# Layer 0 of a convolution-attention kernel: the matrix of scores times ones, by VectorE or by one-column products on TensorE

## The chip, the cores and the metric

One core of one Trainium2 chip. The metric is the device time of one execution in microseconds (us); lower is better. The kernel before takes 2922.1 us, the median of 3 runs (2920.12 to 2923.42).

## The reference, cut to what matters

The model has two layers. Layer 0 is a spectral convolution with attention between the 32 channels ("times") of each of 4 batches; layer 1 is additive attention over tokens and a small mixture of experts. Only a corner of layer 0 is touched:

```
p_attn = jax.nn.softmax(scores, axis=-1)              # (b, head n, t, s)
av = jnp.einsum('bnts,bnsk->bntk', p_attn, vf)        # vf: spectral part + skip part of the values
p = _fno_layer(av, Pcw, Psw, H, W)                    # mixes the 32 heads again
```

Values and the output projection each have a spectral part and a "skip" part, a plain scale per head (`Vsw[n]`, `Psw[n]`). The skip of the skip needs no spectrum: with the per-head product `pv[n] = Vsw[n] * Psw[n]`, image t receives from image s the factor sum over n of `pv[n] * p_attn[n, t, s]`, times the normalization scale of image s. This 32 x 32 matrix of the scores, summed over heads, plus a unit diagonal (the residual `p + xa`), is what the changed function makes. It is applied to the pixels of image s as a product.

## The kernel before, in words

**The stages of layer 0.** The kernel runs layer 0 for 4 batches b (each 32 images of 128 x 128), then layer 1. For each b the order is: the convolution loop (line 963 on), the transform back, statistics, two spectral layers with a GELU, and, still within b, the attention weights of batch b+1 and the last additions of b.

**The convolution loop.** Five blocks of up to 13 rows of modes (`x0`), each with four groups of source images (`i`), so 20 steps per b. Each step loads `xb` by DMA from SyncE's queue (SP) into a ring of four buffers, copies it to PSUM as `xw` on ScalarE (L980), makes four products `u`: one or two on GpSimd (L989, SBUF with SBUF), the rest on VectorE (L993, PSUM with SBUF), in a ring of six buffers (tag `pr`), and TensorE sums them with the scores `pr` into `po` (L926), in the order in which they were made. Between the steps TensorE turns pixels (`pxt`), ScalarE normalizes them (`xq`), and `skip` multiplies them by `bd` (`sk`, L926 too): the first use of `bd`, some 10 us after the loop begins.

**The end of a batch.** `attention_weights(b + 1, ...)` ends in the softmax and the normalized scores `ph` (L755 on GpSimd, 64 partitions: 32 heads for each half of the times). They go to DRAM and back as `pr`. Meanwhile the last additions of batch b run: for each half `a` of the images, `row_products` makes `y` on TensorE (L342), ScalarE copies it as `v` (L356), TensorE makes `four` (L358, two PSUM buffers, tag `b`) and VectorE adds it to the images `x` (L1399). Then x1, the output of the layer, is stored (L1422), and the loop of b+1 begins.

**The function that is changed**, `skip_matrix` (L780), makes `bd` from `ph`. It is called once before the loop over b (for batch 0) and after the first half (`a == 0`) of the last additions for b = 0, 1 and 2. It does this:
- `sel` (L238): a 0/1 matrix `same` that picks partition p's own image, times the normalization scale.
- `cm` (L787): for each half of the times, one product of 32 rows by 512 columns with `pv` broadcast as the weights, so that all 128 partitions get sum over heads of `pv * ph` for every pair (s, t).
- `cd` (L791) and `cp` (L792): VectorE multiplies the 512 columns by `sel` and sums over s, which leaves each partition the row of its own s.
- `cp` (L795): plus `same`. `bd` (L797): spread over four blocks by a mask.

**What sets the order.** A scheduler places the instructions on each engine by its own estimates; `behind(later, earlier)` pins one instruction after another on the same engine. `cm` is pinned behind `inverted`, the last product of the first half. [...]Rings (tags `a`, `b`, `v`, `wide`, `pr`) say which buffers are shared: `cm` is in PSUM tag `a` (two buffers), as are the `po` of the loop; `cd` shares tag `v` (three buffers) with the copies `v`.

Of the kernel before, what the change touches and what calls it, by code (L numbers as in the profile page):

```python
# [7 lines left out]
F32 = mybir.dt.float32  # L8
AF = mybir.ActivationFunctionType
ALU = mybir.AluOpType  # L10
AX = mybir.AxisListType
PSUM = bass.MemoryType.PSUM

P = 128
B, T, H, C = 4, 32, 128, 128
NH = 32
# [20 lines left out]
def _constants():  # L37

    w = np.arange(P)
    kx = np.concatenate([np.arange(32), np.arange(-32, 0)])  # L40
    ky = np.arange(KY)
    th = 2 * np.pi / P
    c, s = np.cos(th * np.outer(w, kx)), np.sin(th * np.outer(w, kx))
    rows = np.concatenate([c, -s], 1)
    inv_rows = np.concatenate([c.T, -s.T], 0)
    angle = th * np.outer(w, ky)
    cc, cs = np.cos(angle), np.sin(angle)

    cols = np.concatenate([cs, 0 * cc[:, :1], cc, cc[:, 32:33], -cs], 1) / NPIX
    along_c = np.concatenate([cc[:, 1:], cs[:, 1:], -cs[:, 1:]], 1) / NPIX  # L50
    twice = np.where(ky == 0, 1.0, 2.0)[:, None]
    re, im = twice * cc.T, -twice * cs.T
    inv_cols = np.concatenate([re, im], 0)
    back = np.tile(2 * np.concatenate([cc.T[1:], cs.T[1:]], 1), (4, 1))
    p = np.arange(P)
    same = (p[:, None] % 32 == np.arange(32)[None, :]).astype(np.float64)
    block = (p[:, None] // 32 == np.arange(4)[None, :]).astype(np.float64)

    eye = np.eye(32)
    comb = np.zeros((4, 32, 3, 32))  # L60
    comb[0, :, 0], comb[3, :, 0] = eye, -eye
    comb[1, :, 1], comb[2, :, 1] = eye, eye
    comb[:, :, 2] = -comb[:, :, 0]
    pairs = np.concatenate([np.tile(eye, (4, 1)), np.concatenate([eye, eye, -eye, -eye])], 1)

    of_cos, of_sin = np.zeros((2, 2, 32, 2, KX))
    k = np.arange(1, 32)
    of_cos[0, 0, 0, 0] = 1
    of_sin[0, 0, 1, 0] = -1
    for m, sign in ((k, 1), (KX - k, -1)):  # L70
        of_cos[0, k, 0, m], of_cos[1, k, 1, m] = 1, sign
        of_sin[1, k, 0, m], of_sin[0, k, 1, m] = sign, -1
    low = np.r_[0:16, 48:64]
    unfold = [
        np.concatenate([-t[:, 1, low], t[:, 0, low], t[:, 1, low], t[:, 0], t[:, 1]], 1)
        for t in (of_cos.reshape(KX, 2, KX), of_sin.reshape(KX, 2, KX))
    ]
    unfold = np.tile(np.concatenate(unfold, 1), (2, 1))
    high = ((p % KX >= 16) & (p % KX < 48)).astype(np.float64)
    edge = np.zeros(P)  # L80
    edge[:KY] = edge[KY + 2 : 2 * KY] = 1
    edge[0] = edge[KY - 1] = 0.5
    no_column = np.where(p % KX == 16, 0, high / 2)
    of_low = np.where(p >= KX, 1, np.where(p % 32 == 16, 1, 0.5))
    halves = np.stack([high, no_column, edge, of_low], 1)

    group = (p[:, None] // 4 == p[None, :] // 4) / (4.0 * NPIX / C * T)
    of_group = p[:, None] // 4 == np.arange(32)[None, :]
    by_p = np.concatenate(
        [rows, inv_rows, cols, unfold, halves, same, block, comb.reshape(P, 96), pairs, group, of_group / 4]  # L90
        + [along_c, back],
        1,
    )
    return by_p.astype(np.float32), inv_cols.astype(np.float32)


NX = 2 + 3 * KY
NU = 3 * 32 + 2 * KX
NY = KY - 1
NCONST = 128 + 128 + NX + 2 * NU + 4 + 32 + 4 + 96 + 64 + P + 32 + 3 * NY + 2 * P  # L100
NM = KX * KY
NK = 13

# [27 lines left out]
def layer0(  # L131
# [12 lines left out]
    def behind(later, earlier):  # L144

        tc.add_manual_dep(
            later.ins,
            earlier.ins.name,
            mybir.DependencyInfo(mybir.DependencyClass.NoSync, mybir.DependencyReason.DATA),
            reason="order",  # L150
        )
# [25 lines left out]
    def columns(n):  # L177
        at[0] += n
        return cst[:, at[0] - n : at[0]]
# [8 lines left out]
    group, of_group = columns(P), columns(32)  # L188
    cos_c, sin_c, minus_sin_c = columns(NY), columns(NY), columns(NY)
    cos_back, sin_back = columns(P), columns(P)  # L190
    par = const.tile([P, NSMALL], F32, name="par")
    nc.sync.dma_start(out=par, in_=small_row.partition_broadcast(P))
    ident = const.tile([P, P], F32, name="ident")
# [35 lines left out]
    def per_image(name):  # L229
        return small.tile([P, T], F32, name=name, tag=name)  # L230

    def scalars(op, name, a, b):

        out = per_image(name)
        if isinstance(b, float) or b.shape[1] == 1:
            nc.vector.tensor_scalar(out, a, b, None, op)
        else:
            nc.vector.tensor_tensor(out, a, b, op)  # L238
        return out
# [94 lines left out]
    def row_products(spec, a, ahead=(), slots=range(4), wide=None):  # L334

        wide = wide or [ps.tile([P, 2, 512], F32, name="y1", tag="wide") for _ in range(2)]
        for slot in slots:
            c = slice(slot * P, slot * P + P)
            for k, trig in enumerate((cos_back, sin_back)):
                for g in range(4):  # L340
                    r = slice(32 * g, 32 * g + 32)
                    mm = nc.tensor.matmul(  # L342
                        wide[g // 2][:, g % 2, c],
                        spec[r, 4 * a + slot, 64 - 64 * k : 192 - 64 * k],
                        trig[r],
                        start=k == 0,
                        stop=k == 1,
                    )
                    for earlier in ahead:
                        behind(mm, earlier)  # L350
        return wide

    def four_images(wide, g, copy, v_ring=dict(tag="v", bufs=3), tag="b"):
# [32 lines left out]
    def one(name, n=1):  # L386
        return small.tile([P, n], F32, name=name, tag=name)
# [391 lines left out]

    def skip_matrix(ph, ysc, earlier=None):  # L780

        cp = per_image("cp")
        sel = scalars(ALU.mult, "sel", same, ysc)
        for h in range(2):
            r = slice(32 * h, 32 * h + 32)
            cm = ps.tile([P, T, 16], F32, name="cm", tag="a")
            mm = nc.tensor.matmul(cm, pv[r].to_broadcast([NH, P]), ph[r], start=True, stop=True)  # L787
            if earlier is not None:
                behind(mm, earlier)
            cd = grp.tile([P, T, 16], F32, name="cd", tag="v", bufs=3)  # L790
            nc.vector.tensor_tensor(cd, cm, sel.unsqueeze(2).to_broadcast([P, T, 16]), ALU.mult)  # L791
            nc.vector.tensor_reduce(  # L792
                cp[:, 16 * h : 16 * h + 16], cd.rearrange("p s t -> p t s"), AX.X, ALU.add
            )
        nc.vector.tensor_add(cp, cp, same)  # L795
        bd = small.tile([P, 4, T], F32, name="bd", tag="bd")
        nc.vector.tensor_tensor(  # L797
            bd,
            block.unsqueeze(2).to_broadcast([P, 4, T]),
            cp.unsqueeze(1).to_broadcast([P, 4, T]),  # L800
            ALU.mult,
        )
        return bd
# [108 lines left out]
    for b in range(B):  # L912
# [480 lines left out]
        for a in HALVES:  # L1393
            groups = [slice(16 * a + g, 16 * a + g + GI) for g in (0, GI)]

            def last(images, four):
                g = images[0] - 16 * a
                to = xr[:, 16 * a : 16 * a + 16].rearrange("p (k t) c -> p k t c", k=2)[:, :, g : g + 2]
                added = nc.vector.tensor_tensor(to, to, four.rearrange("p (k t) c -> p k t c", k=2), ALU.add)  # L1399
                if a == 0:  # L1400
                    behind(added, weights[7])

            def last_scaled(images, four):
                for j, t in enumerate(images):
                    nc.scalar.activation(
                        gl[:, t],
                        four[:, j],
                        AF.Identity,
                        bias=cq[:, t : t + 1],
                        scale=c3[:, t : t + 1],  # L1410
                    )
                for t in (images[0], images[2]):
                    nc.vector.tensor_tensor(xr[:, t : t + 2], xr[:, t : t + 2], gl[:, t : t + 2], ALU.add)

            if b + 1 < B:
                inverted = back(spec, a, last, begun if a == 0 else (), nc.scalar.copy)
            else:
                back(spec, a, last_scaled, apart=True)
            if a == 0 and b + 1 < B:
                bd = skip_matrix(weights[2], front[4], inverted)  # L1420
            for i in groups:
                stored = nc.sync.dma_start(out=x1[b, i].rearrange("t w c -> w t c"), in_=xr[:, i])  # L1422
                if b + 1 < B:
                    behind(stored, weights[3])
# [639 lines left out]
```

## Time and profile before

| | us |
|---|---|
| median of 3 runs | 2922.1 |
| profiled execution, device time | 2926.9 |
| its span in the trace | 2925.1 |
| loop of the first batch, first to last `u` of VectorE | 70.52 to 130.36 |
| loop of the second batch | 267.58 to 323.03 |
| loop of the third batch, start | 458.87 |
| loop of the fourth batch, start | 650.37 |
| `cm` products | 16 records, median 0.640 |
| `cd` | 8, median 0.687 |
| `cp` sums | 8, median 1.022 |
| `cp` plus `same` | 4, 0.179 to 2.067 |
| `bd` | 4, 0.279 to 1.978 |

Everything in layer 0 lies before about 836 us; layer 1 takes the rest. Times in the trace are from the start of the span. One float32 product of the program shows as two records (the 8 `cm` products are 16 records). A row of the timeline gives start, length, engine, line, operation, output and inputs, count, and in brackets how long the engine had been idle and what ended that.

### The profile page before, as it was taken

What the parts mean: (1) busy time and instruction counts of PE and PEld (TensorE: products, weight loads), DVE (VectorE), ACT (ScalarE), POOL (GpSimd) and SP (SyncE); (2) the same over time, 40 slices, a digit from 0 to 9 for tenths busy, and PEclk for the clock granted to TensorE, in tenths of its full rate; (3) what the DMA queues carried; (4) which work ended last, traced back from release to release, by engine and by line L of the source; (5) the groups of instructions that cost most, each with busy time, mean ns of one, the idle gap of its engine ahead of it and who ended that gap; (6) DMA issues with size and microseconds to landing.
All of it is one profiled execution on the core that took longest, in us unless ns stands there. A gap on an engine that the chain in (4) does not pass through costs nothing.

```text
span 2925.1 us, 52645 instructions
## 1 busy us (share of the span) xinstructions
PE 2735.4 (94%) x19506; PEld 1352.7 (46%) x19506; DVE 2189.4 (75%) x4860; ACT 2322.9 (79%) x3243; POOL 2034.0 (70%) x1804
## 2 busy tenths in 40 slices
PE   8898998988878999999899999989999999999997
PEld 5565664655544444334444443434444343444443
DVE  4888788778756777666587787657778776878877
ACT  3556466455469999899899999989999998999991
POOL 1706418146139887878988887898787889798773
PEclk9999999999979999999999999999999999999998
DMA  3304205033020101011000100210000011000000
GB/s 101 123 1 112 78 15 163 13 75 101 19 77 9 25 8 33 8 33 41 19 8 17 24 15 17 49 27 14 24 17 15 19 48 26 15 19 15 15 15 15
DMA packets 151152, 107.71 MB, mean 37 GB/s; under 512 B 36302, under 2 KB 140017, under 8 KB 150897
## 3 DMA queue, kind: packets, MB, share of 16 engines
q1 hardware_dynamic: 147633, 102.26, 13.1%
q8 instruction: 154, 2.52, 0.4%
q10 hardware_dynamic: 3264, 2.10, 0.3%
q14 instruction: 101, 0.83, 0.1%
HBM read 63.86 MB, written 19.50 MB: 28 GB/s over the span
## 4 chain that ended last, share of the span: by engine, by line
PE 47%; POOL 11%; ACT 9%; issue 5%; DVE 5%; DMA 0%; POOLq 0%; SPq 0%; DVEq 0%; ACTq 0%
PE d L1854 20%; PE po L1873 12%; PE px L1760 6%; ACT r L1904 5%; PE n L1854 4%; POOL e L1913 3%; POOL e L1912 3%; ACT e L1920 2%; POOL kx L1519 1%; DVE r L1909 1%; DVE xc L1764 1%; POOL x L1519 1%; PE pl L1738 1%; POOL u L989 1%; ACT r L1916 1%
## 5 line engine op out<-in xcount | busy, mean ns | idle before, releaser
L1909 DVE TENSOR_TENSOR r<-n,r 128x1024 f32<-128x1024 f32 (+1 forms) x1056 | 962.0, 953 | 481.5 <-PE n L1854 397.9
L1912 POOL TENSOR_TENSOR e<-r 128x512 f32<-128x512 f32 x528 | 673.2, 1275 | 273.3 <-DVE r L1909 272.8
L1904 ACT ACTIVATE r<-d 128x1024 f32<-128x1024 f32 (+1 forms) x1056 | 792.9, 802 | 67.4 <-PE n L1854 59.3
L1916 ACT ACTIVATE r<-r 128x1536 f32<-128x1536 f32 x528 | 783.6, 1484 | 16.8
L1913 POOL TENSOR_TENSOR e<-e,r 128x512 f32<-128x512 f32 x528 | 671.3, 1271 | 41.4
L1854 PE MATMUL d<-qe,ke 32*128 32x512 f32 (+3 forms) x2304 | 607.5, 603 | 39.9 <-ACT r L1904 35.8
L1873 PE MATMUL po<-e,kx 128*128 128x512 f32 (+3 forms) x1152 | 594.3, 605 | 17.2 <-POOL e L1925 17.2
L1854 PE MATMUL n<-qe,ke 32*128 32x512 f32 (+3 forms) x2304 | 607.0, 602 | 0.0
L1854 PE MATMUL n<-qf,kf 32*128 32x512 f32 (+3 forms) x2304 | 553.5, 555 | 0.0
L1854 PE MATMUL d<-qf,kf 32*128 32x512 f32 (+3 forms) x2304 | 551.9, 555 | 0.0
L1764 DVE SCALAR_TENSOR_TENSOR xc<-px,wgt,xc 128x128 f32<-128x128 f32 x1024 | 358.4, 351 | 41.4 <-PE px L1760 10.6
L1920 ACT ACTIVATE e<-e 128x512 f32<-128x512 f32 x528 | 325.8, 617 | 66.0 <-POOL e L1913 65.1
L1873 PEld LDWEIGHTS po<-e,kx 128*128 128x128 f32 x1152 | 175.4, 188 | 394.6 <-issue 308.6
L1854 PEld LDWEIGHTS d<-qe,ke 32*128 32x128 f32 x2304 | 177.0, 184 | 360.2 <-ACT r L1904 340.2
L1854 PEld LDWEIGHTS d<-qf,kf 32*128 32x128 f32 x2304 | 220.7, 186 | 177.2 <-issue 164.5
L1760 PE MATMUL px<-we,x2t 128*128 128x512 f32 x512 | 265.9, 605 | 6.8 <-DVE xc L1764 5.5
L989 POOL TENSOR_TENSOR u<-xb,gb 128x858 f32<-128x858 f32 (+1 forms) x112 | 220.5, 2008 | 42.6 <-PE po L926 38.8
L1854 PEld LDWEIGHTS n<-qf,kf 32*128 32x128 f32 x2304 | 228.4, 185 | 18.9 <-issue 11.2
L1140 POOL TENSOR_TENSOR spec<-part,part 128x512 f32<-128x512 f32 x16 | 25.8, 1610 | 286.5 <-DVE gn_r_t L253 93.1
L993 DVE TENSOR_TENSOR u<-xw,gb 128x858 f32<-128x858 f32 (+1 forms) x208 | 215.4, 1100 | 6.8 <-ACT xw L980 3.2
L1854 PEld LDWEIGHTS n<-qe,ke 32*128 32x128 f32 x2304 | 177.9, 183 | 9.4 <-DVE r L1909 0.9
L926 PE MATMUL po<-u,pr 128*32 128x429 f32 (+1 forms) x1280 | 151.2, 532 | 24.9 <-POOL u L989 18.5
(425 smaller groups left out, 3378.4 us busy)
## 6 DMA issues: line engine op xcount, KB each, us to landing
xb<-xd SPq DMA_DIRECT2D x128, 214.5 KB
xc<-x SPq DMA_DIRECT2D x29, 512.0 KB
x<-x SPq DMA_DIRECT2D x16, 512.0 KB
qf<-qe SPq DMA_DIRECT2D x64, 128.0 KB
out<-xc SPq DMA_DIRECT2D x15, 512.0 KB
x<-in_x SPq DMA_DIRECT2D x14, 512.0 KB
xb<-xd SPq DMA_DIRECT2D x32, 198.0 KB
kf<-ke SPq DMA_DIRECT2D x32, 128.0 KB
```

The costliest lines, as they stand in the source:

```text
L989: weighed = nc.gpsimd.tensor_tensor(u, xb, gk, ALU.mult)
L993: weighed_last = nc.vector.tensor_tensor(u, xw, gk, ALU.mult)
L1760: nc.tensor.matmul(px, x2t[:, k * P : (k + 1) * P], we[:, e0 : e0 + 4], start=True, stop=True)
L1764: nc.vector.scalar_tensor_tensor(xc[:, k], px[:, e], wgt[:, k, e0 + e : e0 + e + 1], xc[:, k], ALU.mult, ALU.add)
L1854: nc.tensor.matmul(o, k, q, start=turn == 0 or g > 0, stop=turn == 1 or g > 0)
L1873: nc.tensor.matmul(sums[c, h][:, q0 : q0 + c1 - c0], kx[:, jb], e[:, c0:c1], start=jb == 0, stop=is_last and q0 > 2 * P, skip_group_check= ...
L1904: nc.scalar.activation(r[:, g], d, AF.Ln, scale=1.0 / DSCALE)
L1909: nc.vector.tensor_tensor(r[:, g], part, r[:, g], ALU.mult)
L1912: nc.gpsimd.tensor_tensor(e, r[:, 1], r[:, 2], ALU.add)
L1913: nc.gpsimd.tensor_tensor(e, e, r[:, 0], ALU.add)
L1916: nc.scalar.activation(r, r, AF.Exp, scale=-1.0)
L1920: nc.scalar.activation(e, e, AF.Exp)
```

## The change

The matrix is made in another way and at another time.

- **Products.** For each half of the times, 16 products replace one: the weights are the 32 x 32 scores of one time t (read with a stride of 16 elements), the moving operand is the single column `pv`, and the result goes to 32 partitions and one column of `cm`, 128 x 4. All float32.
- **Selecting.** `by_four` (VectorE, 16 columns, twice) multiplies the 4 columns by the block mask. One product with a new constant 128 x 128 matrix `alike` (ones where p and q belong to the same image modulo 32) brings the sums to all partitions, in PSUM, as `cp[:, 0]`.
- **Scale and diagonal.** `own`, a sum of `sel` over its row, is each partition's scale; one VectorE instruction makes `cp[:, 1] = cp[:, 0] * own + same`, in PSUM. `bd` then reads it there.
- **Constants.** `alike` makes the table of constants 128 columns wider (1517 to 1645 columns, loaded once at the start).
- **Order.** For b = 0, 1, 2 the function is called in the second half (`a == 1`), its products pinned behind the last `y` product of that half; in the compiled order 13 of the 32 one-column products stand ahead of the half's four `four` products and 19 after them, then the product with `alike`, then the first `po`. On VectorE the order becomes: additions 1 to 3 of the second half, the first `u`, addition 4, `by_four` twice, the second `u`, `cp`, the third `u`, `bd`. For the first batch: `by_four` twice ahead of the first `u`, `cp` after it, `bd` after the second. ScalarE's, GpSimd's and SP's orders are unchanged.

```diff
+    by_p = np.concatenate([by_p, np.tile(same, (1, 4))], 1)
...
+    alike = columns(P)
...
     def row_products(spec, a, ahead=(), slots=range(4), wide=None):
...
+        roots["rows"] = mm
         return wide
...
     def skip_matrix(ph, ysc, earlier=None):
 
-        cp = per_image("cp")
         sel = scalars(ALU.mult, "sel", same, ysc)
+        own = one("own")
+        nc.vector.tensor_reduce(own, sel, AX.X, ALU.add)
+        by_four = small.tile([P, 2, 4, 4], F32, name="by_four", tag="cp")
         for h in range(2):
             r = slice(32 * h, 32 * h + 32)
-            cm = ps.tile([P, T, 16], F32, name="cm", tag="a")
-            mm = nc.tensor.matmul(cm, pv[r].to_broadcast([NH, P]), ph[r], start=True, stop=True)
-            if earlier is not None:
-                behind(mm, earlier)
-            cd = grp.tile([P, T, 16], F32, name="cd", tag="v", bufs=3)
-            nc.vector.tensor_tensor(cd, cm, sel.unsqueeze(2).to_broadcast([P, T, 16]), ALU.mult)
-            nc.vector.tensor_reduce(
-                cp[:, 16 * h : 16 * h + 16], cd.rearrange("p s t -> p t s"), AX.X, ALU.add
+            cm = ps.tile([P, 4], F32, name="cm", tag="a")
+            for t in range(16):
+                j = 32 * (t % 4)
+                mm = nc.tensor.matmul(
+                    cm[j : j + 32, t // 4 : t // 4 + 1], ph[r, :, t], pv[r], start=True, stop=True
+                )
+                if earlier is not None:
+                    behind(mm, earlier)
+            nc.vector.tensor_tensor(
+                by_four[:, h],
+                block.unsqueeze(1).to_broadcast([P, 4, 4]),
+                cm.unsqueeze(2).to_broadcast([P, 4, 4]),
+                ALU.mult,
             )
-        nc.vector.tensor_add(cp, cp, same)
+        cp = ps.tile([P, 2, T], F32, name="cp", tag="a")
+        nc.tensor.matmul(cp[:, 0], alike, by_four.rearrange("p h k j -> p (h k j)"), start=True, stop=True)
+        nc.vector.scalar_tensor_tensor(cp[:, 1], cp[:, 0], own, same, ALU.mult, ALU.add)
         bd = small.tile([P, 4, T], F32, name="bd", tag="bd")
...
-            cp.unsqueeze(1).to_broadcast([P, 4, T]),
+            cp[:, 1].unsqueeze(1).to_broadcast([P, 4, T]),
...
             if b + 1 < B:
-                inverted = back(spec, a, last, begun if a == 0 else (), nc.scalar.copy)
+                if a:
+                    begun = [row_products(spec, a)]
+                    rows_last = roots["rows"]
+                inverted = back(spec, a, last, begun, nc.scalar.copy)
...
-            if a == 0 and b + 1 < B:
-                bd = skip_matrix(weights[2], front[4], inverted)
+            if a and b + 1 < B:
+                bd = skip_matrix(weights[2], front[4], rows_last)
```

More of the change, by code (lines that the diff above doesn't have):

```diff
@@ L99 @@
 NY = KY - 1
-NCONST = 128 + 128 + NX + 2 * NU + 4 + 32 + 4 + 96 + 64 + P + 32 + 3 * NY + 2 * P
+NCONST = P + 128 + 128 + NX + 2 * NU + 4 + 32 + 4 + 96 + 64 + P + 32 + 3 * NY + 2 * P
 NM = KX * KY
```

## The prediction

> **What bounds the kernel now.** I read the page first, then the order of events around the end of each image of layer 0. "Boundary" below is the stretch from the last L1399 additions of image b to the first products of image b+1.
>
> ```profile
> span 2925.1 us, 52645 instructions
> ...
> L989 POOL TENSOR_TENSOR u<-xb,gb 128x858 f32<-128x858 f32 (+1 forms) x112 | 220.5, 2008 | 42.6 <-PE po L926 38.8
> ...
> L993 DVE TENSOR_TENSOR u<-xw,gb 128x858 f32<-128x858 f32 (+1 forms) x208 | 215.4, 1100 | 6.8 <-ACT xw L980 3.2
> ```
>
> The two rows are the halves of one loop, 4 images x 20 steps: VectorE makes 52 `u` per image and sits idle 6.8 us before 208 of them; GpSimd makes 28 and waits 42.6 us, nearly all for PE. So the loop runs at VectorE's pace. VectorE's timeline at the first boundary (start us, length us) shows why the loop starts late:
>
> ```profile
> 258.13 0.69 DVE L1399 TENSOR_TENSOR x<-x,four 128x512 f32<-128x512 f32 x1 [0.17 <-PE four L358]
> 259.25 0.69 DVE L791 TENSOR_TENSOR cd<-cm,sel 128x512 f32<-128x512 f32 x1 [0.43 <-PE cm L787]
> 259.98 1.02 DVE L792 TENSOR_REDUCE cp<-cd 128x16 f32<-128x512 f32 x1
> 260.91 0.69 DVE L791 TENSOR_TENSOR cd<-cm,sel 128x512 f32<-128x512 f32 x1
> 261.63 1.04 DVE L792 TENSOR_REDUCE cp<-cd 128x16 f32<-128x512 f32 x1
> 262.71 2.07 DVE L795 TENSOR_TENSOR cp<-cp,cst 128x32 f32<-128x32 f32 x1
> 264.81 0.29 DVE L797 TENSOR_TENSOR bd<-cst,cp 128x128 f32<-128x128 f32 x1
> 265.02 1.28 DVE L1399 TENSOR_TENSOR x<-x,four 128x512 f32<-128x512 f32 x2
> 266.98 0.69 DVE L1399 TENSOR_TENSOR x<-x,four 128x512 f32<-128x512 f32 x1 [0.68 <-PE four L358]
> 267.58 1.04 DVE L993 TENSOR_TENSOR u<-xw,gb 128x858 f32<-128x858 f32 x1
> 268.55 0.68 DVE L1399 TENSOR_TENSOR x<-x,four 128x512 f32<-128x512 f32 x1
> 269.14 36.94 DVE L993 TENSOR_TENSOR u<-xw,gb 128x858 f32<-128x858 f32 x35
> ```
>
> `bd` takes VectorE from 259.25 to 265.1 and stands ahead of the additions of the second half; then 35 `u` follow without a gap, 1.055 us each. The other engines in the same windows:
>
> ```profile
> 258.02 1.09 PE L787 MATMUL cm<-ph,pv 32*128 32x512 f32 x2
> ...
> 258.98 2.12 PE L342 MATMUL y<-cst,spec 32*128 32x128 f32 x52
> ...
> 261.20 1.07 ACT L356 COPY v<-y 128x512 f32<-128x512 f32 x2 [5.66 <-PE y L342]
> ...
> 267.73 1.87 PE L926 MATMUL po<-u,pr 128*32 128x429 f32 x8
> ...
> 268.80 2.01 POOL L989 TENSOR_TENSOR u<-xb,gb 128x858 f32<-128x858 f32 x1 [4.08 <-PE po L926]
> ```
>
> PE's `y` products run among the `cm` products and end at 261.10; ScalarE waits for them. The first `po` comes at 267.73, GpSimd's third `u` 1.07 us later.
>
> [...] L795 (both inputs SBUF) took 0.18 us at its shortest and 2.07 above, beside a GpSimd `u`; at the other two boundaries `bd` was hit (1.98). The changed `by_four`, `cp` and `bd` each have one tensor in PSUM, so I price no stall. [...] This trace shows no one-column product; I price it by the 64-column ones.
>
> ```profile
> 236.37 1.08 PE L679 MATMUL so<-xx 128*32 128x64 f32 x26 [0.35 <-DVE xx L550]
> ```
> ```profile
> 326.14 7.13 PE L1027 MATMUL py<-cst,rs 128*64 128x64 f32 x115 [0.61 <-ACT rs L1013]
> ```
>
> A product is two records. L679 (32 weight columns read with a stride, as the new `cm`) gives (1.08-0.31)/25 = 31 ns a record; 0.31 is one record's length. L1027 (64 strided columns) gives (7.13-0.28)/114 = 60 ns. I take 31, and keep 60 as the upper bound[...].
>
> **The change part by part.**
>
> *Products.* Per image 2 `cm` products of 512 columns go (4 records, some 0.44 us apart, 1.8 us of PE) and 32 of one column come: 64 x 31 ns = 2.0 us. In the compiled order they stand behind the `y` products: 13 before the four `four`, 19 after, then `cp`. The 13 (26 records, 0.8 us) fill the 0.73 us in which PE waits for `v` anyway: 0 to 0.1 us. The 19 take 38 x 31 ns = 1.2 us.
>
> *VectorE.* Gone at this boundary: 0.69+1.02+0.69+1.04+2.07+0.29 = 5.8 us. Added: two `by_four` and `cp` at 0.17 each (0.18 for a 67x32 product with PSUM, L571), `bd` 0.29: 0.8 us. `own` (0.19) lies behind `sel`, under a wait for ScalarE's logarithm of 0.5 us: nothing; without that cover 0.6 us in all.
>
> *What is late next.* Rebuilt boundary: PE is free for `y` at 258.0; 60 records at 36 ns end at 260.15 (0.95 earlier, no `cm` between). `v` at 260.25; `four` 0.63 later (as 261.20 to 261.83), 260.9; additions 1.13 after (as 265.85 to 266.98): first 262.0, second 262.9. `four` 3 and 4 wait for their two PSUM buffers: 262.8 and 263.7. Third addition 263.9; first `u` 264.5 (its `xw` is copied by 263.7); fourth addition 265.5. The 19 `cm` start at 264.6, end 265.8; `by_four` 266.15 to 266.5; second `u` 266.5 (was 269.14). `cp` product 266.7, first `po` about 266.9 (was 267.73: 0.8 earlier). Then third `u`, `bd`, fourth `u` at 269.0; before it was 269.14 + 2 x 1.055 = 271.25. VectorE leads by 2.2; I take 2.1.
>
> *Does the lead last?* GpSimd's third `u` gains only 0.8, its fourth (271.25, waiting for the `po` of VectorE's second) 1.2. From there it is dense to 281.26, then waits 0.53, 0.21 and 1.80 us for PE, which waits for VectorE. The missing 0.9 us fits in these 2.5 us, so the 2.1 stand at the end. The second boundary is alike (449.62 to 460.43, where this one has 258.13 to 269.14). At the third, two loads of layer 1's input (L1539, 1 MB) share the queue and the chain runs from GpSimd's `u` ending at 662.2 through a transfer 663.70 to 669.51: there only GpSimd's 1.25 us count. The stores of x1 move up with the additions; they stand ahead of the `xb` loads on SP, so these are not held by it.
>
> *First image.* Gone: 3.7 us of VectorE (71.49 to 76.8, between `u`); added 0.8, and VectorE now waits for the 64 records: 69.75 + 2.0 + 0.2 = 71.95. Second `u` 73.45 (was 74.52), fourth 75.75 (was 76.74): 1.0 us; `po` 0.3 later, before GpSimd's wait of 2.0.
>
> *Constant matrix.* 64 KB more in a start-up that moves about 300 GB/s: 0.2 us lost.
>
> Sum: 1.0 + 2.1 + 2.1 + 1.25 - 0.2 = 6.2 us of the profiled execution's 2926.9 (span 2925.1 and 1.8 around it), which is 0.16% above the median shown. 2922.1 x (1 - 6.2/2926.9) = 2915.9.
>
> **Rivals.** (A) GpSimd becomes the bound: only the lead of `po` counts, 3 x 0.8 - 0.3 - 0.2 = 1.9 us, 2920.2. For: it is busy 18.2 of 20 us in the loop, dense from 271.25 to 281.26. Against: the 2.5 us of waits above. (B) Slower: the strided weight loads. At 60 ns a record PE spends 64 x 29 ns = 1.86 us more per image, on the way `y`, `cm`, `four`, `by_four`, `cp`, `po`: 4 x 1.86 - 6.2 = 1.2 us lost, 2923.3. It decides from 55 ns a record (6.2 us / 256 records = 24 above 31); 0.2% slower needs 78. Against: L679. (C) More: all the net VectorE time lands, 3 x 5.0 + 2.9 - 0.2 = 17.7 us, 2904.4; it would need `y` to end far earlier, so I expect at most half, some 2912 to 2908.
>
> **How the numbers follow.** This kernel's measurement tells about 0.2% (5.8 us) from no change. Forecast 0.52, own range 2913 to 2918 [...]; 0.33 of it beyond 0.2%, which lies at 2916.3. A 0.20, B 0.14 (0.08 beyond 0.2% slower, since a one-column product with 32 rows is not in the trace), C 0.14. Faster 0.33 + 0.14 = 0.47, same 0.19 + 0.20 + 0.06 = 0.45, slower 0.08. The range, 2908.5 to 2924, holds A and B's priced case and leaves out the far half of C and of B.
>
> **What would show it.** Right: `y` ending some 2.1 us after it starts, VectorE's fourth `u` about 2 us sooner after the last first-half addition (now 13.1 us), `bd` never near 2 us, `cm` records near 31 ns apart. Wrong: a wait of VectorE for `cm` above 0.3 us at a boundary, or of PE for `by_four` above 1 us (C and the forecast fall, B rises); a GpSimd without waits through steps 1 to 10 (A).

## The result and the profile after

| | us |
|---|---|
| before, median of 20 runs | 2922.49 (2920.12 to 2924.19) |
| after, median of 20 runs | 2915.69 (2911.25 to 2920.68) |
| ratio after / before | 0.9979, 95% interval 0.9972 to 0.9986 |
| profiled execution of after, its span | 2917.0, 2915.3 |

The kernel is 6.8 us faster; the interval is 4.1 to 8.2 us. The prediction was 2915.9. The sum was right, but its terms were wrong in opposite directions: the first batch gave far more than predicted, the three boundaries less. What follows is mostly about those terms.

The lines of the page that answer to the three of before (the last number before the arrow is the idle time ahead of the group):

```profile
span 2915.3 us, 53131 instructions
...
L1001 POOL TENSOR_TENSOR u<-xb,gb 128x858 f32<-128x858 f32 (+1 forms) x112 | 221.0, 2017 | 33.8 <-PE po L938 29.1
...
L1005 DVE TENSOR_TENSOR u<-xw,gb 128x858 f32<-128x858 f32 (+1 forms) x208 | 217.3, 1109 | 7.2 <-ACT xw L992 3.5
```

GpSimd's `u` lost 8.8 us of waiting (42.6 to 33.8); VectorE's wait is the same as before (6.8 and 7.2). So the loop still runs dense on VectorE, and starts earlier. VectorE's timeline at the first boundary:

```profile
257.88 1.47 DVE L1411 TENSOR_TENSOR x<-x,four 128x512 f32<-128x512 f32 x2 [3.04 <-PE four L361]
259.85 0.69 DVE L1411 TENSOR_TENSOR x<-x,four 128x512 f32<-128x512 f32 x1 [0.49 <-PE four L361]
260.46 1.04 DVE L1005 TENSOR_TENSOR u<-xw,gb 128x858 f32<-128x858 f32 x1
261.42 0.68 DVE L1411 TENSOR_TENSOR x<-x,four 128x512 f32<-128x512 f32 x1
262.01 0.24 DVE L799 TENSOR_TENSOR by_four<-cst,cm 128x16 f32<-128x16 f32 x2
262.18 1.04 DVE L1005 TENSOR_TENSOR u<-xw,gb 128x858 f32<-128x858 f32 x1
263.14 0.25 DVE L807 SCALAR_TENSOR_TENSOR cp<-cp,own,cst 128x32 f32<-128x32 f32 x1
263.30 1.04 DVE L1005 TENSOR_TENSOR u<-xw,gb 128x858 f32<-128x858 f32 x1
264.25 0.28 DVE L809 TENSOR_TENSOR bd<-cst,cp 128x128 f32<-128x128 f32 x1
264.45 12.50 DVE L1005 TENSOR_TENSOR u<-xw,gb 128x858 f32<-128x858 f32 x12
```

The last first-half addition started at 254.15 here and at 258.13 before, so the fourth `u` (264.45; before 271.06) comes 10.3 us after it instead of 12.9. (The prediction put it at 271.25 before, by the mean spacing of 1.055; the `u` at the start of that row are 0.96 apart.) `bd` and `cp` take 0.28 and 0.25 us, with no stall. TensorE in the same stretch:

```profile
254.05 2.05 PE L344 MATMUL y<-cst,spec 32*128 32x128 f32 x60
256.03 0.65 PE L794 MATMUL cm<-pv,ph 32*32 32x1 f32 x26
256.65 4.02 PE L361 MATMUL four<-v,cst 128*128 128x512 f32 x8
260.60 0.70 PE L794 MATMUL cm<-pv,ph 32*32 32x1 f32 x38
262.31 0.41 PE L806 MATMUL cp<-by_four,cst 128*128 128x32 f32 x2 [1.01 <-DVE by_four L799]
262.65 2.67 PE L938 MATMUL po<-u,pr 128*32 128x429 f32 x20
```

`y` ends 2.05 us after it starts and 26 `cm` records lie in the wait for `v`; the other 38 end at 261.3, and TensorE then waits 1.01 us until VectorE has done the fourth addition and `by_four`. And GpSimd, whose dense run starts earlier, but whose last two waits stay what they were (0.21 and 1.80 before):

```profile
263.72 18.76 POOL L1001 TENSOR_TENSOR u<-xb,gb 128x858 f32<-128x858 f32 x9 [2.96 <-PE po L938]
282.69 3.49 POOL L1001 TENSOR_TENSOR u<-xb,gb 128x858 f32<-128x858 f32 x2 [0.21 <-PE po L938]
287.94 18.20 POOL L1001 TENSOR_TENSOR u<-xb,gb 128x858 f32<-128x858 f32 x9 [1.76 <-PE po L938]
```

**Where the time came from.** What follows the last loop differs by up to 5.5 us from profile to profile, and the start by 2 us, so single executions are compared by four stages instead: from VectorE's softmax sum (`sm`, L749 before, L752 after) of a batch to the end of that batch's last `u`.

| stage, us | batch 0 | 1 | 2 | 3 |
|---|---|---|---|---|
| before | 73.95 | 68.89 | 68.70 | 69.33 |
| after | 69.68 | 67.19 | 67.12 | 68.59 |
| gain | 4.27 | 1.70 | 1.58 | 0.74 |
| predicted | 1.0 | 2.1 | 2.1 | 1.25 |

The sum of the gains is 8.3 us; after starts its first stage 0.3 us later and loses 0.2 more between the stages, so that at the end of the last loop it leads by 7.75 us, inside the interval of the runs.

Kernels that share the code of a stage show how far one profile can be trusted. The first two boundaries of before, e1 and e12 (below) take 68.63 to 68.89 us, the first batch of the seven kernels that have the new one unchanged 69.58 to 69.74. The last stage scatters far more: 69.33, 70.72 and 73.04 in before, e12 and e1. So the gains of the first three batches are clear, and the 0.74 of the last is one draw.

### The profile page after: what moved, and what is told of

Same layout as the page of the kernel before. It is cut to its first block, busy times and chain, and to the rows that moved or that the text cites. A ratio compares the mean times of both kernels' runs of the same rounds, so it can differ in the third digit from the quotient of the medians.

```text
span 2915.3 us, 53131 instructions
## 1 busy us (share of the span) xinstructions
PE 2731.0 (94%) x19754; PEld 1349.5 (46%) x19754; DVE 2173.9 (75%) x4856; ACT 2323.5 (80%) x3243; POOL 2034.6 (70%) x1804
## 4 chain that ended last, share of the span: by engine, by line
PE 60%; POOL 14%; ACT 11%; DVE 9%; issue 5%; DMA 0%; POOLq 0%; SPq 0%; DVEq 0%; ACTq 0%
PE d L1869 21%; PE po L1888 12%; PE px L1775 6%; ACT r L1919 4%; PE n L1869 4%; POOL e L1928 3%; POOL u L1001 3%; POOL e L1927 3%; PE po L938 2%; ACT e L1935 2%; POOL kx L1534 2%; PE pz L307 2%; DVE r L1924 2%; PE px L1135 1%; DVE xc L1779 1%
## 5 line engine op out<-in xcount | busy, mean ns | idle before, releaser
L1001 POOL TENSOR_TENSOR u<-xb,gb 128x858 f32<-128x858 f32 (+1 forms) x112 | 221.0, 2017 | 33.8 <-PE po L938 29.1
```

Of the source, the lines that this page charges most:

```text
L1001: weighed = nc.gpsimd.tensor_tensor(u, xb, gk, ALU.mult)
```

## The experiments

Each kernel starts from the kernel after, unless its line says otherwise. Stages are those of the table.

**1. The first batch alone** (e1_first_only): the new function for batch 0, the old one at its old place for the boundaries.

```diff
...
-                if a:
-                    begun = [row_products(spec, a)]
-                    rows_last = roots["rows"]
-                inverted = back(spec, a, last, begun, nc.scalar.copy)
+                inverted = back(spec, a, last, begun if a == 0 else (), nc.scalar.copy)
-            if a and b + 1 < B:
-                bd = skip_matrix(weights[2], front[4], rows_last)
+            if a == 0 and b + 1 < B:
+                bd = skip_matrix_old(weights[2], front[4], inverted)
```

> The new way for the first batch only; for the other three boundaries the old way at the old place. Theory now (from the two traces): the first batch alone gains about 4.3 us at its loop's end, because the one-column products take 14 to 18 ns a record and hide under VectorE's last copy of gb, and 0.33 us go at the start; the boundaries then repeat the times of before. So 2918.5 of 2922.5, ratio 0.9986, and a lead over before of 3.9 to 4.0 us at the first sum of every batch. Rival (the prediction's own terms): the first batch gives 0.8 us, ratio 0.9997, and what looks like its gain in the trace of after comes from elsewhere.

Measured: 2919.26 us, ratio 0.9994 (0.9985 to 1.0002): by the time alone nothing is decided. The stages decide: 69.58, 68.63, 68.63, 73.04. The first gains 4.37 as in the kernel after, the second and third 0.26 and 0.07, which is the noise of unchanged code. The fourth, unchanged too, is 3.7 us longer: VectorE waits up to 2.55 us for late transfers there, and TensorE's clock falls to 0.50 at 668.9 us (experiments 5 and 6).

**2. Method and place apart.** e2_old_place makes the matrix in the new way where the old one stood (`a == 0`); e3_old_method makes it in the old way at the new place.

```diff
e2:
+                inverted = back(spec, a, last, begun if a == 0 else (), nc.scalar.copy)
+            if a == 0 and b + 1 < B:
+                bd = skip_matrix(weights[2], front[4], inverted)
e3:
...
-    bd = skip_matrix(weights[2], front[4])
+    bd = skip_matrix_old(weights[2], front[4])
...
-                bd = skip_matrix(weights[2], front[4], rows_last)
+                bd = skip_matrix_old(weights[2], front[4], rows_last)
```

> The new way everywhere, but called after the first half of the additions as before, so by_four, cp and bd stand ahead of the second half's additions on VectorE. Theory: most of the boundary's gain is the VectorE time that is gone (5.8 us against 0.8), wherever it stands; each boundary still gains 1 to 2 us, total 2914 to 2918. Rival (the place does it: the additions come first, so the four products and the first po come early): no gain at the boundaries, only the first batch's 3.9 us, 2918.5.

> The old way (512-column products, VectorE's sums) everywhere, but called after the last y products of the second half, so the additions come first. Theory: the first batch gains nothing; at the boundaries the additions end some 5 us sooner, but VectorE's 5.8 us then stand among the first u products, where VectorE and GpSimd are both busy, so each boundary gains between -1 and +1 us: 2919 to 2925. Rival (the place does it): about 1.5 us gained at each boundary, 2918.

Measured: e2 2913.43 us, ratio 0.9971 (0.9961 to 0.9981), stages 69.62, 67.39, 67.33, 68.07. e3 2924.8 us, ratio 1.0011 (1.0005 to 1.0018), stages 73.55, 68.89, 68.68, 74.17. The move by itself gains 0.00 and 0.02 us at the first two boundaries; the new method gains 1.50 and 1.37 there without the move. So the method does it. The 0.2 us by which after is ahead of e2 there are no more than unchanged code differs by (0.26 in e1), so a gain of the place is not shown. Nor does e3 tell why the move gains nothing with the old method: at each of these two boundaries the granted clock stood at 0.50 for 3.4 us (experiment 6), and at the first GpSimd waited 2.85 us for `xb`. Its total came out as expected partly because the last stage lost 4.8 us, which was not expected.

**3. Who is the bound behind a boundary?** One `u` per batch of 1 to 3, in the first block, is moved: from GpSimd to VectorE (e6_u_to_vector), or from VectorE to GpSimd (e10_u_to_gpsimd).

```diff
-                        if ri == 0 and (k == 0 or i == 1 or i == 3 and x0 // NK % 2 == 0):
e6:
+                        if ri == 0 and (k == 0 or i == 1 or i == 3 and x0 // NK % 2 == 0 and (x0 or b == 0)):
e10:
+                        if ri == 0 and (k == 0 or i == 1 or i == 3 and x0 // NK % 2 == 0 or i == 2 and x0 == 0 and b):
```

> The changed kernel, with one u product of the first block of batches 1, 2 and 3 (step 4, the one that GpSimd makes for the second half of the times) moved from GpSimd to VectorE. Theory (after the change GpSimd bounds the first nine steps of the loop: its nine u from 263.72 to 282.48 have no gap): the loop ends 0.3 to 1.0 us sooner in batches 1 and 2; 2913 to 2915 against 2915.7. Rival (VectorE still bounds it, as the prediction had it): VectorE's 1.05 us more are lost in each, 2919.

> The changed kernel, with one u product of the first block of batches 1, 2 and 3 (step 3, second half of the times) moved from VectorE to GpSimd: 7 instead of 6 for GpSimd there. If GpSimd bounds the first nine steps after the change (its u have no gap there): the loops of batches 1 and 2 end 1.5 to 2.0 us later than in the changed kernel, the boundary's gain of 1.6 to 1.7 is used up. If VectorE bounds it, as the prediction had it: they end up to 1 us sooner, since VectorE has 1.04 us less.

Measured: e6 2915.14 us, ratio 0.9975 (0.9966 to 0.9985), stages of batches 1 and 2 67.09 and 67.23. e10 2919.61 us, ratio 0.9993 (0.9984 to 1.0001), stages 70.40 and 70.33, 3.2 later. So e6 met neither expectation: 1.05 us more of VectorE and 2 us less of GpSimd changed the stages by 0.1 us. An estimate fits it: by the timelines VectorE's fourth `u` leads by 2.64 us after the change and GpSimd's by 1.6; with one more `u` VectorE's lead is 1.6 too. Both engines are within about a `u` of being the bound. With e10 GpSimd has too much and VectorE waits:

```profile
279.62 5.64 DVE L1005 TENSOR_TENSOR u<-xw,gb 128x858 f32<-128x858 f32 x5 [1.35 <-PE po L938]
```

(In e10 TensorE's clock also fell to 0.50, from 274.2 to 277.6 and likewise in the other two batches. How much of the 3.2 is due to that was not separated; experiment 6.)

**4. The price of a one-column product.** e4_cm_four issues each product four times in a row; e11_cm_four_rounds goes four times through the 16 of a half, so that neighbours write different groups of 32 partitions. Both make the same sums again.

```diff
e4:
             for t in range(16):
                 j = 32 * (t % 4)
+                for _ in range(4):
e11:
-            for t in range(16):
+            for t in 4 * list(range(16)):
```

> The changed kernel with each one-column product issued four times (the same product into the same place, 128 instead of 32 for each batch; the result is the same). Theory (14 to 18 ns a record, and nearly all on the way to by_four and po): 192 more records for each batch, 2.7 to 3.4 us; the loop's end moves back by 2 to 3 us in every batch, some 8 to 12 us in all, so 2924 to 2928 against 2915.7. If a record cost 31 ns on the way, as the prediction took it: 24 us, 2939. If the products lie hidden beside other waits: under 2 us.

> As the run with each one-column product issued four times, but in another order: the round of 16 products[...] is made four times, so that neighbours never share a position. There the 256 records of the first batch came 34 ns apart, with four neighbours in one position; in the changed kernel 64 come 12 to 15 ns apart. If the position decides: 256 records in the first batch take some 4 us (15 ns). If the rate of instructions decides (a burst of waiting instructions goes fast, a longer stream does not): again 30 to 36 ns a record, some 8 us, with a fast start at most.

Measured: e4 2945.75 us, ratio 1.0082 (1.0067 to 1.0097), slower than either number expected; e11, in a single run, 2936.7. The first batch in TensorE's timeline, e4 and then e11:

```profile
69.47 8.84 PE L795 MATMUL cm<-pv,ph 32*32 32x1 f32 x256
```
```profile
69.82 2.48 PE L794 MATMUL cm<-pv,ph 32*32 32x1 f32 x161
73.22 1.63 PE L794 MATMUL cm<-pv,ph 32*32 32x1 f32 x95 [0.91 <-issue]
```

8.84/256 is 34 ns a record, 2.48/161 is 15 ns and 1.63/95 is 17. A fast start is not the reason, for at the second boundary 230 records follow each other in both (e4 first):

```profile
468.19 7.88 PE L795 MATMUL cm<-pv,ph 32*32 32x1 f32 x230
```
```profile
462.29 3.50 PE L794 MATMUL cm<-pv,ph 32*32 32x1 f32 x230
```

That is 34 ns a record against 15. So the price went with the order of the products: 34 ns a record where four in a row were the same product, with the same weights into the same 32 partitions and column of `cm`, and 15 to 17 where neighbours wrote different groups of 32 partitions. No run separates the weights from the place. The change itself cycles through the groups, as e11 does. So the expectation of e4 failed by its own edit: it did not keep what it was to multiply.

**5. Layer 1's transfer in the last stage** (e5_prefetch_late; e9_old_place_prefetch is the same edit on e2): the two 0.5 MB loads of layer 1's first images are pinned behind the last `xb` load.

```diff
-        nc.sync.dma_start(out=xc, in_=x1[b, i0 : i0 + NB].rearrange("t w c -> w t c"))
+        read = nc.sync.dma_start(out=xc, in_=x1[b, i0 : i0 + NB].rearrange("t w c -> w t c"))
+        if not pools:
+            behind(read)
...
-            first((ps, images))
+            first((ps, images, lambda read: behind(read, broadcast)))
```

> The changed kernel with the two loads of layer 1's first input (1 MB) pinned behind the last load of xb in the last batch. Theory (the last boundary gains less, 0.74 us, because these loads hold back xb, and VectorE waits 1.50 us for it): the last batch's loop ends 1 to 2 us sooner, so its gain is 1.7 to 2.5, and the total is 2914. Rival (that boundary is limited by GpSimd like the others and the loads only fill free time): within 0.3 us of the changed kernel, or later, since layer 1 begins later.

> The new way at the old place (as the run with the old place, 2913.4) with layer 1's first loads pinned behind the last load of xb. Theory: both gains add, 1 to 2 us below the old place alone, 2911.5 to 2912.5. Rival: the loads weren't in the way there (VectorE waited 0.72 us), no difference: 2913.4.

Measured: e5 2914.52 us, ratio 0.9977 (0.9966 to 0.9987), last stage 67.19, a gain of 2.14 instead of 0.74; the others as in after. e9 2912.83 us, ratio 0.9971 (0.9959 to 0.9982), last stage 67.51 (e2 68.07). In the kernel after, VectorE's last loop stands still here, behind an `xw` whose `xb` is late:

```profile
662.30 19.43 DVE L1005 TENSOR_TENSOR u<-xw,gb 128x858 f32<-128x858 f32 x18 [1.50 <-ACT xw L992]
```

GpSimd waits 1.45 and 0.48 us for `xb` beside it. With e5 both waits for transfers are gone, and the 1.40 us by which its stage is shorter are about the 1.50 of this wait. The loads need not be pinned for that: in e6, where GpSimd has one `u` less in this batch too, GpSimd waits 1.3 us for `xb`, VectorE hardly, and the stage takes 67.11. A late `xb` also comes without these loads: in e9's third batch GpSimd waits 0.97 us for one, and that stage is 0.75 longer than in e2. e9 has the lowest median of all, but its interval overlaps those of after and e2: no version is shown to beat the kernel after, and e9's expectation is not decided.

**6. The granted clock in the first batch.** The gain of 4.27 us was not explained by VectorE, whose fourth `u` comes only 2.65 us earlier in its stage. VectorE in the first batch, before and then after (its fourth `u` is the first of the row at 76.74, and the second of the row at 73.46, at 74.42):

```profile
71.49 1.28 DVE L791 TENSOR_TENSOR cd<-cm,sel 128x512 f32<-128x512 f32 x2
72.69 1.92 DVE L792 TENSOR_REDUCE cp<-cd 128x16 f32<-128x512 f32 x2
76.74 5.84 DVE L993 TENSOR_TENSOR u<-xw,gb 128x858 f32<-128x858 f32 x6
```
```profile
70.82 0.45 DVE L799 TENSOR_TENSOR by_four<-cst,cm 128x16 f32<-128x16 f32 x2
73.46 12.69 DVE L1005 TENSOR_TENSOR u<-xw,gb 128x858 f32<-128x858 f32 x13
```

TensorE's windows and timeline of the kernel before (columns of the window: length, busy and records, granted clock, DMA share, GB/s):

```profile
77.00:78.00 1.00, 1.00 (x10) 0.50 0.51 166
```
```profile
72.28 0.93 PE L926 MATMUL po<-u,pr 128*32 128x429 f32 x8 [1.40 <-issue]
75.62 4.85 PE L926 MATMUL po<-u,pr 128*32 128x429 f32 x22 [2.42 <-DVE u L993]
```

While VectorE makes `cd` and `cp`, TensorE waits 1.40 and 2.42 us. Within the second wait its clock falls to 0.50, where it stays from 74.2 to 81, and 22 `po` records take 4.85 us; 22 others at 81.89, at 1.00, take 2.33. In the kernel after the clock is 1.00 throughout this stage. So products that nobody reads were put into the waits: one 128 x 512 product ahead of the first `po` and two after it in the kernel before (e12_before_filled), and two into the wait that a long `bd` makes (e13_stall_filled, from experiment 7).

```diff
+        def fill(n):
+
+            idle = ps.tile([P, 512], F32, name="idle", tag="b")
+            for _ in range(n):
+                product(idle, ident, cst[:, :512], start=True, stop=True)
e12:
-        mixed = [inverted] if b else []
+        mixed = [inverted] if b else [roots["cm"]]
...
+        if b == 0:
+            fill(1)
         rs = big.tile([P, KX, KY], F32, name=f"rs_{b}", tag="rs")
...
                     for j in range(4):
                         product(
...
+                        if b == 0 and x0 == 0 and i == 0 and (k, j) == (0, 3):
+                            fill(2)
e13:
+                        if b == 0 and x0 == 0 and i == 0 and (k, j) == (1, 1):
+                            fill(2)
```

> The kernel before with three products added for TensorE in the first batch alone, 128 x 512, that nobody reads: one ahead of the first po, two in the 2.42 us in which TensorE waits for VectorE after it. VectorE's work stays as before, 3.7 us of it between its u. Theory: the first stage of the kernel before lost some 2 us beyond VectorE's own lead because TensorE stood idle for 3.8 of 4.7 us and its granted clock was 0.50 from 74.2 to 81. With the filler the clock stays at 1.00 through 74 to 81, the 22 po records from 75.6 on take about 2.3 us instead of 4.85, and the first stage, 73.95 us before and 69.68 with the change, takes 71.5 to 72.5. Rival: the clock cost nothing since TensorE has slack, and the stage stays at 73.5 to 74.

> The kernel with cp in SBUF, whose bd takes 1.6 us, with two filler products (128 x 512, read by nobody) in the 1.75 us in which TensorE waits for VectorE behind bd, in the first batch alone. There the first stage took 72.41 us against 69.68 with the change, 2.7 more for a bd that is 1.35 longer, and the clock was 0.50 from 74.7 to 78. Theory: with the filler the clock stays at 1.00 and the stage takes 70.7 to 71.3, the 1.35 us alone. Rival: the stall costs its 2.7 us by VectorE's and GpSimd's order alone, and the stage stays at 72.2 to 72.6.

e12, the same two views:

```profile
77.00:78.00 1.00, 0.96 (x12) 1.00 0.46 172
```
```profile
72.27 1.98 PE L927 MATMUL idle<-cst,ident 128*128 128x512 f32 x4
74.79 1.99 PE L927 MATMUL po<-u,pr 128*32 128x429 f32 x12 [0.53 <-DVE u L1002]
```

The first stage takes 72.46 us instead of 73.95 in e12 (2922.0 in a single run), and 71.22 instead of 72.41 in e13 (2916.4 in a single run), with the clock at 1.00 in both. VectorE's early instructions are unchanged in e12, from the first `u` to `bd`, to 0.04 us. A second profile of the old method in the first batch, e3, has 73.55 us, with the clock at 0.50 as well. So these two stages were 1.19 us (e13) and 1.49 us (e12) shorter at the full clock, and e12's 1.09 shorter than e3's, though TensorE was waiting for others; each figure is from one profile.

In the traces of before and after every change of the clock (37 and 29 of them) lies on a grid of 3.41 us, whose place differs between the two. The steps in e7 (experiment 7), the first two in the first batch, the others at the first boundary; the second column is TensorE's busy time:

```profile
71.28:74.69 3.41, 1.48 (x12) 1.00 0.29 95
74.69:78.10 3.41, 3.41 (x29) 0.50 0.51 178
265.84:269.25 3.41, 2.43 (x20) 1.00 0.93 255
269.25:272.66 3.41, 2.68 (x50) 1.00 0.81 248
```

TensorE was busy for 1.48 us of the first step, with a wait of 1.75 us in it, and the next step is at 0.50. The wait of 1.57 us at the boundary, from 268.37 to 269.94, lies 0.88 us in one step and 0.69 in the next, busy for 2.43 and 2.68 us, and the clock stays at 1.00. In the traces of before and after, from 20 us on, each of the 13 full-speed steps with TensorE's records in less than 0.44 of the time is followed by one at 0.50, 19 of the 89 between 0.44 and 0.70, and none of the 1,544 above 0.70. (In before the step from 70.80 to 74.21 has 0.29; in e10 TensorE was busy for 1.86 of the 4 us from 270 to 274, ahead of the fall at 274.2.) This is a regularity of these two traces, and the streams of one-column products of e4 and e11 depart from it: there the clock fell to 0.50 at 73.7 and 73.4 us, in e4 after 4.2 us without a gap, in e11 with one gap of 0.91. What decides between 0.44 and 0.70 stays open.

**7. The stall of `bd`** (e7_cp_in_sbuf): `cp` goes to SBUF, so that `bd` has two inputs there.

```diff
-        nc.vector.scalar_tensor_tensor(cp[:, 1], cp[:, 0], own, same, ALU.mult, ALU.add)
+        cps = per_image("cps")
+        nc.vector.scalar_tensor_tensor(cps, cp[:, 0], own, same, ALU.mult, ALU.add)
...
-            cp[:, 1].unsqueeze(1).to_broadcast([P, 4, T]),
+            cps.unsqueeze(1).to_broadcast([P, 4, T]),
```

> The changed kernel with the sums cp written to SBUF instead of PSUM, so that bd on VectorE has two SBUF inputs while GpSimd makes its u. Theory (the stall of up to 2 us that cp and bd had before comes from two SBUF inputs beside a GpSimd instruction): bd takes 1 to 2 us in at least two of the batches 1, 2 and 3 instead of 0.28; since GpSimd bounds the steps after it, only part shows at the loop's end, 0 to 1 us each: 2916 to 2918. Rival (the stall belonged to the place, beside GpSimd's first u): bd stays at 0.28 us and the time within noise of 2915.7.

Measured: 2918.03 us, ratio to before 0.9984 (0.9977 to 0.9991), an interval that overlaps that of after. All four `bd` of e7 (shortest, median, longest in ns):

```profile
L810 DVE TENSOR_TENSOR bd<-cst,cps x4: 1619/1624/1783, 71.3 to 647.5; 128x128 f32<-128x128 f32 x4
```

In the kernel after they take 277 to 278. The stall ended with a `u` of GpSimd. At the first boundary, GpSimd's row and then VectorE's:

```profile
266.78 4.03 POOL L1002 TENSOR_TENSOR u<-xb,gb 128x858 f32<-128x858 f32 x2 [2.94 <-PE po L939]
```
```profile
267.31 1.62 DVE L810 TENSOR_TENSOR bd<-cst,cps 128x128 f32<-128x128 f32 x1
```

GpSimd's first `u` of this row ends at 268.78, `bd` at 268.93. In before three instructions of `skip_matrix` stalled, `cp` at 262.71 (2.07 us) and `bd` at 454.41 and 645.91 (1.98 each): they end 0.05, 0.15 and 0.15 us after a `u` of GpSimd that began before them or, for `cp`, 0.02 us after it did. Where `bd` began 0.09 us ahead of GpSimd's `u` (e12 at 75.71), it took 0.28. The stages are 72.41, 67.62, 67.60 and 69.31, so 2.73, 0.43, 0.48 and 0.72 later than after. At the first two boundaries two thirds of the 1.35 us are covered, which fits that GpSimd is late there as well (experiment 3); in the first batch twice as much is lost, 1.19 us of it gone when the clock stays at 1.00 (e13, experiment 6).

## Why the prediction came out, point by point

**The bound.** That VectorE's 35 dense `u` set the pace was right for the loop, and too simple for its first steps: there GpSimd is as late (experiment 3).

**Products.** Predicted 31 ns a record; measured (0.70 - 0.20)/37 = 14 at the boundary and (0.97 - 0.20)/63 = 12 in the first batch, 0.20 being one record's length. The row I priced by, L679, has 64 columns, not one; that one column would take as long was my estimate, and no run had shown it. At the boundary the error cost nothing: the 38 records end 0.7 us before VectorE comes to `by_four`.

**VectorE's part and the stall.** Right: 0.24 + 0.25 + 0.28 us where 0.8 was predicted, and no `bd` near 2 us. That an operand in PSUM spares the stall was an estimate when it was priced; the trace of before has a case of it, `cd` with `cm` in PSUM, 0.69 us at 260.91 beside a `u` of GpSimd. e7 shows it for `bd`: with two SBUF inputs it took 1.62 to 1.78 us, with `cp` in PSUM 0.28.

**What is late next.** Right but for 0.3 to 0.4 us: VectorE leads by 2.64 us at the fourth `u` (predicted 2.2), the first `po` by 1.1 (0.8), GpSimd's fourth `u` by 1.6 (1.2).

**Does the lead last?** This step failed. It said that GpSimd's waits of 0.53, 0.21 and 1.80 us are "for PE, which waits for VectorE", so that the missing 0.9 us "fits in these 2.5 us, so the 2.1 stand at the end". The trace of before shows otherwise. In this loop TensorE waits almost only for GpSimd (total us, times, longest; 268 to 323 us):

```profile
PE po L926 <- POOL u L989: 3.4, 6, 0.9
PE po L926 <- DVE u L993: 0.6, 1, 0.6
```

Its one wait for VectorE comes at 270.24, ahead of GpSimd's dense run; in the stretch of the three waits it waits for GpSimd alone, 0.61 us at 283.69. So they were no slack for GpSimd to catch up in: only the 0.53 went, the others are 0.21 and 1.76 after. The stages gained 1.70 and 1.58, which is GpSimd's 1.6, not VectorE's 2.64. Rival A had the mechanism; it went wrong on the size, since it gave GpSimd only 0.8. That GpSimd holds back the rest is borne out by e10, but with so little room that one `u` changes it (e6).

**The third boundary.** 1.25 was predicted by the transfer's chain, 0.74 measured, and in this profile the transfer holds the stage back: with the two loads out of the way the gain is 2.14 (e5). But the stage scatters by more than the term: in e3 and e1 it was 4.8 and 3.7 us longer than before, with VectorE waiting for transfers; that these are the same two loads was not tested there. So the miss of 0.5 says little.

**First image.** Predicted 1.0, measured 4.27: the term that was most in error. Its first part is a price: VectorE was to wait for the `cm` products until 71.95, but they were made by 71.05, under the last copy of `gb`. The fourth `u` came 2.65 us earlier in its stage instead of 1.0. The second part was in no step: the granted clock, without whose fall the stage of before was 1.49 us shorter (e12). With 1.49 for it 0.1 remains (4.27 - 2.65 - 1.49), within the noise. I had not read the clock by windows, where 0.50 stood in the kernel before. It fell at 74.21, after a step of 3.41 us in which TensorE was busy for 1.00: two waits lie in it, the 1.40 and the first 1.01 of the 2.42. In e7 it fell after a step with one wait of 1.75.

**Constant matrix.** The 0.2 us (64 KB at the 291 to 368 GB/s that before moved from 4 to 12 us) could not be seen: the softmax sum of batch 0 lies at 54.8 to 56.7 us in the twelve profiles of kernels that all load the matrix at the start. An experiment on it was not tried.

**The rivals.** B fell with the price per record. Its sign, TensorE waiting over 1 us for `by_four`, did appear (1.01 us), and meant the opposite: TensorE was early, not VectorE. C would have needed all of VectorE's time; of its 5.0 us at a boundary 1.6 land.

**The sum.** The terms were off by -0.9 us at the first two boundaries, -0.5 at the third and +3.3 in the first batch. The four stages therefore gained 8.3 us where 6.4 were predicted for them (6.2 with the constant matrix). The medians differ by 6.8, with 4.1 to 8.2 as the interval, so they cannot tell the two sums apart; that the forecast lies only 0.2 us from the median is in part luck.

## What to carry to other kernels

When a wait on one engine falls away, follow the lead along every engine that feeds the same consumer; here the smallest lead is what arrived. Before counting waits further down as slack, look up whom the engine that they are for is waiting for itself. When an engine that others depend on stands idle, look at its granted clock in the windows after the gap: the gap's price can go on after the gap (in before 22 `po` records took 4.85 us at 0.50, and 2.33 at 1.00). Where a product is very small, vary the order of the places it writes before pricing it (15 and 34 ns a record here). And compare stages of the same code first: they show which gains one profile can carry.

## What the runs showed of the hardware that was not expected

- One-column float32 products with 32 x 32 weights came 12 to 17 ns a record apart when neighbours wrote different groups of 32 partitions (after and e11; 15 over 230 records), 34 ns when four in a row were the same product (e4).
- A dense stream of them did not keep TensorE's clock up: in e4 it fell to 0.50 at 73.7 us, after 4.2 us without a gap, and in e11 at 73.4, 3.6 us into the stream with one gap of 0.91.
- In before and after the clock changed only on a grid of 3.41 us (66 changes), and each of the 13 full-speed steps with TensorE's records in less than 0.44 of it was followed by one at 0.50. In before it fell after 2.41 us of waiting inside one step, in e7 after 1.75; in e7 it stayed at 1.00 through a wait of 1.57 us that lay 0.88 us in one step and 0.69 in the next.
- With products that nobody reads in the waits the clock was at 1.00 where it had been at 0.50 (e12, e13), and the stages show no cost of them: 72.46 us instead of 73.95, and 71.22 instead of 72.41.
- The instructions of VectorE with both inputs in SBUF that stalled behind a `u` of GpSimd ended 0.05 to 0.15 us after that `u` (three in before, `bd` at the first boundary of e7), and took 1.34 to 1.50 us longer in e7 (1.62 to 1.78 against the 0.28 of after) and 1.7 to 1.9 in before (`bd` 1.98 against 0.28, `cp` 2.07 against 0.18).
